# A two-layer graph network: row sums on quarters of TensorE's array, edge products on halves of it

## The chip, the core and the metric

One Trainium2 chip, one of its cores. A core has five engines that run side by side: TensorE (PE, matrix products into PSUM; its weight loads are PEld), VectorE (DVE), ScalarE (ACT), GpSimd (POOL, which here issues the indirect DMAs, that is gathers and scatters by an index list) and SyncE (SP, which issues the plain DMAs). The metric is the time of one execution in microseconds (us).

## What is computed

A graph of 1250 nodes with 512 features and 40000 edges, sorted by target node. First layer: graph attention with 8 heads of 64 features, then a dense block. Second layer: edge features are mixed into the messages, which are summed, then two dense layers with a normalisation over the nodes. Cut to what matters:

```python
# first layer
h  = layer_norm(x) * ln1_g + ln1_b
xl, xr = (h @ Wl).reshape(-1, 8, 64), (h @ Wr).reshape(-1, 8, 64)
e  = einsum('ehc,hc->eh', leaky_relu(xl[src] + xr[dst], 0.2), att)
ex = exp(e - segment_max(e, dst)[dst])
alpha = ex / (segment_sum(ex, dst)[dst] + 1e-16)
x1 = x + segment_sum(alpha[..., None] * xl[src], dst).reshape(-1, 512) + gat_bias
x1 = x1 + gelu((layer_norm(x1) * ln2_g + ln2_b) @ W1 + b1) @ W2 + b2
x  = layernorm(x + x1)
# second layer
msg = relu(x[src] + edge_attr @ W_e + b_e)
h   = (1 + eps) * x + segment_sum(msg, dst)
h   = silu(batch_norm(h @ W1 + b1)) @ W2 + b2
out = layernorm(x + silu(batch_norm(h)))
```

All of it is in float32.

## The kernel before

**Blocks and rows.** The nodes are ranked by degree and put in ten blocks of 128, one node per SBUF partition. Block b has `KB[b]` slots (44 in block 0 down to 25 in block 9, 333 in all). One slot of a block is one gathered "row": a POOL instruction (`get`, `gather`) that fetches, for each of the 128 nodes, the 512 features of its neighbour in that slot. Each layer gathers 333 such rows.

**Recorded order.** In the first layer and the preparation all engines are called through `inorder`, which makes the instructions of an engine run in the order of the program. All those instructions carry one line, L783, so they are told apart by their tiles. The second layer's edge part calls the engines directly and has lines of its own.

**Preparation** (to about 85 us): weights are turned and permuted, the left features `xl` are written to a table in HBM, ranks and index lists are made. Its last steps turn the permutation that is to be undone later (`pu_` into `undo`), permute the bias (`pg`), form the last block's product (`product(9)`, `taken(9)`, `lin(8, 9)`), and form the negated right features of block 9 (`xn` to `xT` to `nxr9`).

**First layer, attention** (about 100 to 905 us). A block's rows come in groups of at most 20 (`GN`), 21 groups, and a group in chunks of at most 5 rows (`CN`), 75 chunks. A chunk has one buffer `xg`; there are seven (`GB`). For each chunk, in the loop over groups and chunks:

- `scores`: POOL gathers the chunk's rows into `xg`; DVE takes maximum and minimum with `nxr` into `z`, multiplies by a sign and reduces to the scores `S`. After a group's last chunk `softmax` forms the weights `w`.
- `weigh`, for one chunk of the group before: ACT multiplies about half of the rows by the weights, head by head, DVE the other rows in one product (`xg<-xg,w`); `add_up` then sums the rows, one PE matmul per row with the identity as weights, into the PSUM tile `pacc` (two buffers). Between the rows' sums `part` puts a step of another block's dense layer (`body_of`).
- `merge`, one group later still, adds the group's sum to the block's accumulator `acc` with the softmax correction.
- At a block's first group `normed_of` gathers the next block's node rows into `xn` (one buffer) at the end of the first chunk, and `xr_of`, from the third chunk on, makes the next `nxr` (two buffers) of it. `slots_of` gathers the next block's index list `s_n`.

A chunk's `xg` buffer is free for new gathers when the sums of its rows are done.

**Dense block of the first layer.** `head_of` normalises and turns a finished block, `body_of` does 16 pairs of products: `pu` (four 128x128 matmuls, then GELU on ACT into `uT`) and `py` (one 128x512 matmul, accumulated in PSUM; two buffers), with `end_of` to add, normalise and scatter the result. Their steps are dealt out by `part`, `step_others` and `step_lates`; what remains is done behind the attention (the tail, about 905 to 985 us).

**Second layer, edge part** (about 985 to 1460 us). The features of a block's edges come in one or two gathers `ea` of at most 28 slots (`spans`, `features_of`). `turn` transposes eight slots at a time, two per 128 partitions. `edges` handles rows in pairs: POOL gathers two rows `xs`; PE forms both edge products `pe`, each from all 128 partitions with a weight tile `we` whose other half is zero; DVE adds `pe` to `xs` (L1747) and, in a second instruction, takes the maximum with 0 and adds to the sum `pd` in PSUM (L1748). Between pairs `first_dense` does the next dense layer for finished blocks (`pz`, L1704). `pe` has two buffers, `xs` nine.

**End** (to 1578 us): normalisations over nodes, second dense layer, scatter of the output.

A second function, `general_path`, is compiled beside it for inputs that this plan does not cover. It doesn't run here.

Of the kernel before, what the change touches and what calls it, by code (L numbers as in the profile page):

```python
# [725 lines left out]
def gnn_kernel(ctx, tc, x, src, dst, edge_attr, ln1_g, ln1_b, Wl, Wr, att, gat_bias,  # L726
# [44 lines left out]
    def inverse_std(rs, var):  # L771

        nc.scalar.activation(rs, var, AF.Sqrt, bias=ln_eps[:rs.shape[0]])
        nc.vector.reciprocal(rs, rs)
# [40 lines left out]
    with ExitStack() as s0:  # L815
# [121 lines left out]
        orders = [order, *(kl.tile([P, KD, P], F32, name=f"order{i}") for i in range(2))]  # L937
# [251 lines left out]
        pu_ = lq.tile([P, KD, P], F32, name="pt1")  # L1189
        for k in range(KD):  # L1190
            T.transpose(pu_[:, k, :], orders[2][:, k, :], ident)
        A.copy(sgn, q_b.rearrange("p (h c) -> p h c", c=CH)[:, :, LEFT:RIGHT])
        A.copy(undo, pu_)
        pg = kq.tile([P, KD], F32, name="pg", tag="s")
        for k in range(KD):
            T.matmul(pg[:, k:k + 1], order[:, k, :], cols[:, 68 + k:69 + k], start=True, stop=True)
        A.copy(gcols, pg)
        A.mul(ncols, cols[:, 52:60], -1.0)
# [3 lines left out]

        pt = lq.tile([P, KD, P], F32, name="pt1")
        for k in range(KD):
            T.transpose(pt[:, k, :], xn[:, k * P:(k + 1) * P], ident)
        for k in range(KD):
            A.activation(xT[:, k, :], pt[:, k, :], AF.Identity,
                         scale=ncols[:, k:k + 1], bias=ncols[:, KD + k:KD + k + 1])
# [9 lines left out]
        A.copy(nxr9[:, :, 1:], pm.rearrange("p k n -> p (k n)").rearrange("p (h c) -> p h c", c=CH))  # L1218

    def short_path():  # L1220
        with ExitStack() as sa:
            fast = sa.enter_context(tc.tile_pool(name="fast", bufs=1))
            fdram = sa.enter_context(tc.tile_pool(name="fdram", bufs=1, space=DRAM))
            xb_t = fdram.tile([N + 1, D], F32, name="xb_t")
            xo_t = fdram.tile([NP, D], F32, name="xo_t")
            eps1 = row(eps, 1, "eps1", fast)
            nc.vector.tensor_scalar(eps1, eps1, 1.0, None, op0=OP.add)
            back = fast.tile([P, P], F32, name="back")
            nc.vector.tensor_scalar(back, jp, float(-V0), None, op0=OP.is_equal)
            lone = fast.tile([P, 1], F32, name="lone")  # L1230
            nc.vector.tensor_scalar(lone, jp[:, 0:1], float(-VN), -0.1 * BIG, op0=OP.is_le, op1=OP.mult)
            s2 = sa.enter_context(ExitStack())
            early = {}
            with ExitStack() as s1:
                V, A, T = attention(s1, xb_t, xo_t, back, lone, lambda: begin(s2, early))
            second(s2, early, xb_t, xo_t, eps1, back, V, A, T)

    def attention(s1, xb_t, xo_t, back, lone, follow):
# [26 lines left out]
        V.memset(one, 1.0)  # L1265
        w1 = ap.tile([P, KD, FF], F32, name="w1")
# [35 lines left out]
        def xr_of(blk):  # L1302

            yield from place()
            pt = aq.tile([P, KD, P], F32, name="pt1", tag="pu", bufs=4)
            for k in range(KD):
                T.transpose(pt[:, k, :], blk["xn"][:, k * P:(k + 1) * P], ident)
            yield
            xT = bp.tile([P, KD, P], F32, name="xT", tag="t")
            for k in range(KD):  # L1310
                A.activation(xT[:, k, :], pt[:, k, :], AF.Identity,
                             scale=ncols[:, k:k + 1], bias=ncols[:, KD + k:KD + k + 1])
            held["ps"] -= 1
            yield from place()
            pm = aq.tile([P, D], F32, name="pm", tag="pu", bufs=4)
            for k in range(KD):
                T.matmul(pm, xT[:, k, :], wr[:, k, :], start=(k == 0), stop=(k == KD - 1))
            yield
            blk["nxr"] = nxr = bp.tile([P, HEADS, CX], F32, name="nxr", bufs=2)
            A.copy(nxr[:, :, 1:], heads(pm))  # L1320
            held["ps"] -= 1
            V.memset(nxr[:, :, 0:1], -NEG)
# [24 lines left out]
        held = dict(acc=0, hT=0, head=0, h=0, ps=0)  # L1347
# [62 lines left out]
        def body_of(b, y, hT):  # L1410

            py = aq.tile([P, D], F32, name="py", bufs=2)
# [20 lines left out]
        def end_of(b, y, py):  # L1433

            yield
            V.tensor_add(y, y, py)
            xo = bp.tile([P, D], F32, name="xo")
# [35 lines left out]
        def part():  # L1473

            if not going and ready:
                going.append(body_of(*ready.pop(0)))
            if going and next(going[0], 0) == 0:
                going.pop()
# [44 lines left out]
        def add_up(g, j):  # L1523
            T.matmul(heads(g["pacc"]), ident, row_of(g, j), start=(j == 0), stop=(j == g["n"] - 1))

        def weigh(g):
# [4 lines left out]
            g["pacc"] = aq.tile([P, D], F32, name="pacc", bufs=2)  # L1531
            for c, (c0, cn) in enumerate(g["cuts"]):
# [3 lines left out]
                for j in range(c0, c0 + cn):  # L1536
                    if j < c0 + na:
                        xv = row_of(g, j)
                        for h in range(HEADS):
                            A.activation(xv[:, h, :], xv[:, h, :], AF.Copy, scale=w[:, j, h:h + 1])  # L1540
                    if g["quota"] > 0:
                        g["quota"] -= 1
                        part()
                    add_up(g, j)
                yield

# [56 lines left out]
        for i, g in enumerate(groups):  # L1603
# [9 lines left out]
            g["S"] = sp.tile([P, GN + 1, HEADS], F32, name="S")  # L1613
            nc_ = len(g["cuts"])
            for c in range(nc_):
# [3 lines left out]
                if c == 0:  # L1619
                    if not i:  # L1620
                        others.append(wr_order())
                    if g["first"] and g["b"] != ORDER[-1]:
                        others.append(slots_of(g["b"] - 1))
                        ahead = normed_of(g["b"] - 1)
# [3 lines left out]
                if c == min(1, nc_ - 1) and merging:  # L1628
                    merge(merging)
                if c == 2 and g["first"] and ahead:  # L1630
                    others.append(xr_of(ahead))
                step_others()
                todo = 0
# [3 lines left out]
                for _ in range(todo):  # L1637
                    before["quota"] = quota
                    next(weighing, 0)
                    quota = before["quota"]  # L1640
                for _ in range(quota):
                    part()
                step_lates()
            merging, before = before, g
        merge(merging)
# [4 lines left out]
        follow()  # L1650
        merge(before)
# [6 lines left out]
    def begin(s2, early):  # L1658
# [3 lines left out]
        early["we"] = we = er.tile([P, 2, D], F32, name="we")  # L1662
        nc.gpsimd.memset(we, 0.0)
        nc.sync.dma_start(we[0:ED, 0, :], W_e)
        nc.sync.dma_start(we[ED:P, 1, :], W_e)
        early["features"] = [features_of(ep, *u) for u in spans[:2]]
# [5 lines left out]
    spans = [(b, e0, en) for b in (NB - 1, *range(NB - 1)) for e0, en in parts(KB[b], 28)]  # L1672

    def features_of(ep, b, e0, en):

        wx = w_i[:, b:b + 1]
        if e0:
            wx = ep.tile([P, 1], I32, name="wx")
            nc.vector.tensor_scalar(wx, w_i[:, b:b + 1], float(e0), None, op0=OP.add)
        ea = ep.tile([P, 28 * ED], F32, name="ea", bufs=3)  # L1680
        gather(ea[:, :en * ED], edge_attr, wx)
        return ea

    def second(s2, early, xb_t, xo_t, eps1, back, V, A, T):
# [25 lines left out]
        with ExitStack() as s3:  # L1710
# [3 lines left out]
            pend = {u: ea for u, ea in zip(spans, early["features"])}  # L1714

            def turn(b, e0, en, c0, cn, act=nc.scalar):

                at = spans.index((b, e0, en))
                if c0 == 0:
                    for u in spans[at:at + 2]:  # L1720
                        if u not in pend:
                            pend[u] = features_of(ep, *u)
                ea = pend[b, e0, en]
# [12 lines left out]
            def edges(b, at0, cn, eaT, pd):  # L1736
                for j in range(0, cn, 2):
# [4 lines left out]
                    pe = eq.tile([P, 2, D], F32, name="pe")  # L1742
                    for i in range(m):
                        kk = P if m == 2 else ED
                        nc.tensor.matmul(pe[:, i, :], eaT[:kk, j // 2, :], we[:kk, i, :], start=True, stop=True)  # L1745
                    xv = xs[:, :m, :]
                    add = nc.vector.tensor_add(xv, xv, pe[:, :m, :])  # L1747
                    nc.vector.scalar_tensor_tensor(pd[:, :m, :], xv, 0.0, pd[:, :m, :], op0=OP.max, op1=OP.add)  # L1748
                    if at0 == KO[NB - 1] and j == 2:
                        for k in (NB - 1, *range(NB - 1)):  # L1750
# [15 lines left out]
            units = [(b, e0, en, c0, min(8, en - c0)) for b, e0, en in spans for c0 in range(0, en, 8)]  # L1766
            todo, work = [], None
            eaT = turn(*units[0], A)
            for n, (b, e0, en, c0, cn) in enumerate(units):
                if e0 == 0 and c0 == 0:  # L1770
# [4 lines left out]
                    else:  # L1775
                        (nc.vector if n else V).memset(pd, 0.0)
                ahead = turn(*units[n + 1], nc.scalar if n else A) if n + 1 < len(units) else None
                for _ in edges(b, KO[b] + e0 + c0, cn, eaT, pd):
# [5 lines left out]
                if e0 + c0 + cn == KB[b]:  # L1784
# [131 lines left out]
```

## Time and profile before

| | |
|---|---|
| median of 17 runs | 1579.13 us (1571.07 to 1583.69) |
| profiled execution | 1580.21 us |
| its span, first to last instruction | 1578.4 us |
| mean granted TensorE clock | 0.911 |
| busy: PE, PEld, DVE, ACT, POOL | 1291.4, 673.5, 1177.4, 655.7, 817.5 us |
| row sums `pacc<-xg,ident` | 666 passes, 373.8 us busy, 136.9 us idle before them |
| row gathers `xg`, then `xs` | 333 each, 408.8 and 314.9 us busy on POOL |
| edge products `pe<-we,eaT` | 666 passes, 329.1 us busy |

How to read it: a group is one kind of instruction, `out<-in`, with its count and busy time; "idle before, releaser" is time in which the engine stood, and what ended it. A float32 matmul appears as two passes, each with its weight load. Matmuls overlap their neighbours' ends, so the mean of one is longer than the distance between starts. A wait for several things is put down to the one that came last by the profile, which can be wrong where that engine had long been done. The chain of waits is followed back from the last instruction.

### The profile page before, as it was taken

Reading aid. Unit: us, or ns where it says so; the run is one execution under the profiler, and the core shown is the slowest. Engines: PE = TensorE matmul, PEld = TensorE weight load, DVE = VectorE, ACT = ScalarE, POOL = GpSimd, SP = SyncE. Lnnn points to the kernel's source line nnn. Section 1 sums busy time; section 2 is a strip of 40 time slices with the busy share of each in tenths; the row PEclk is TensorE's granted clock in tenths of the full one; section 3 lists DMA queues with packets and bytes.
Section 4 is the critical chain, followed back from the end, with each engine's and each line's share of the span. In section 5 each row is a group of like instructions: output and inputs, shape, how many; then the busy total and the mean of one; then the engine's idle time right before and its main releaser. Section 6 shows DMA issues by size and latency. Waiting matters only on the chain.

```text
span 1578.4 us, 14337 instructions
## 1 busy us (share of the span) xinstructions
PE 1291.4 (82%) x4290; PEld 673.5 (43%) x4290; DVE 1177.4 (75%) x1494; ACT 655.7 (42%) x1980; POOL 817.5 (52%) x762
## 2 busy tenths in 40 slices
PE   7836668979889798887969898888878999898893
PEld 4422224545545354443525465333323354344552
DVE  7768798687787778789796511899999789969133
ACT  5425365557756556666657542000000111011433
POOL 2368565544464646474664101777777767743002
PEclk9968678989999899897989999899999999999897
DMA  6257754323443534454443131877777767743001
GB/s 234 70 158 249 258 149 112 106 82 108 120 124 112 146 99 139 115 149 116 120 138 108 57 128 51 279 236 212 225 224 224 217 182 212 225 136 108 0 0 67
DMA packets 74597, 228.66 MB, mean 145 GB/s; under 512 B 14750, under 2 KB 15236, under 8 KB 73999
## 3 DMA queue, kind: packets, MB, share of 16 engines
q0 software_dynamic: 60000, 199.10, 42.9%
q1 hardware_dynamic: 14511, 28.56, 5.0%
q8 instruction: 36, 0.59, 0.1%
q14 instruction: 50, 0.41, 0.1%
HBM read 214.68 MB, written 13.05 MB: 144 GB/s over the span
## 4 chain that ended last, share of the span: by engine, by line
PE 41%; DVE 20%; issue 13%; DMA 11%; ACT 10%; POOL 4%; POOLq 0%; DVEq 0%; SPq 0%; ACTq 0%
PE pacc L783 14%; PE pu L783 6%; DVE pd L1748 5%; ACT xg L783 5%; PE pz L783 5%; PE py L783 5%; DMA xs<-xb_t,src_i 5%; DVE z L783 4%; PE pe L1745 4%; DMA xg<-xl_t,src_i 3%; DVE xs L1747 3%; DVE S L783 3%; PE pm L783 3%; PE pz L1704 3%; POOL xs L749 2%
## 5 line engine op out<-in xcount | busy, mean ns | idle before, releaser
L783 POOL DMA_INDIRECT xg<-xl_t,src_i x333 | 408.8, 1228 | 340.5 <-issue 190.1
L783 PE MATMUL pacc<-xg,ident 128*128 128x512 f32 x666 | 373.8, 685 | 136.9 <-ACT xg L783 126.7
L749 POOL DMA_INDIRECT xs<-xb_t,src_i x333 | 314.9, 946 | 126.7 <-issue 65.8
L1745 PE MATMUL pe<-we,eaT 128*128 128x512 f32 x666 | 329.1, 626 | 36.5 <-DVE xs L1747 35.6
L783 ACT ACTIVATE xg<-xg,w 128x64 f32<-128x64 f32 x1328 | 329.0, 341 | 0.0
L783 DVE TENSOR_TENSOR z<-xg,nxr 128x1440 f32<-128x1440 f32 (+4 forms) x150 | 197.1, 1355 | 110.5 <-DMA xg<-xl_t,src_i 110.4
L783 PEld LDWEIGHTS pacc<-xg,ident 128*128 128x128 f32 x666 | 134.2, 215 | 327.9 <-ACT xg L783 202.8
L1747 DVE TENSOR_TENSOR xs<-xs,pe 128x1024 f32<-128x1024 f32 (+1 forms) x170 | 202.1, 1191 | 33.0 <-DMA xs<-xb_t,src_i 19.5
L1745 PEld LDWEIGHTS pe<-we,eaT 128*128 128x128 f32 x666 | 120.4, 197 | 203.6 <-issue 108.3
L783 PEld LDWEIGHTS pu<-hT,w 128*128 128x128 f32 x1280 | 173.3, 200 | 74.7 <-issue 65.7
L1748 DVE SCALAR_TENSOR_TENSOR pd<-xs,pd 128x1024 f32<-128x1024 f32 (+1 forms) x170 | 203.9, 1199 | 1.3
L783 DVE TENSOR_REDUCE S<-z 128x40 f32<-128x2600 f32 (+2 forms) x75 | 191.8, 2558 | 2.6
L783 PE MATMUL pu<-hT,w 128*128 128x128 f32 x1280 | 176.8, 284 | 0.2 <-DVE oacc L783 0.2
L783 PE MATMUL py<-w,uT 128*128 128x512 f32 x320 | 163.7, 596 | 0.0
L783 ACT ACT_TABLE_LOAD x71 | 91.1, 1283 | 30.7 <-DVE S L783 24.3
L783 DVE TENSOR_TENSOR xg<-xg,w 128x1024 f32<-128x1024 f32 (+2 forms) x75 | 99.9, 1335 | 0.0
L783 ACT ACTIVATE uT<-pu,cols 128x128 f32<-128x128 f32 x160 | 56.3, 363 | 96.9 <-PE pu L783 96.0
L1731 ACT COPY eaT<-pt 128x512 f32<-128x512 f32 (+3 forms) x44 | 23.5, 534 | 173.0 <-PE pe L1745 145.6
L783 DVE TENSOR_TENSOR z<-z,sgn 128x960 f32<-128x960 f32 (+2 forms) x75 | 77.8, 1038 | 0.0
L783 PE MATMUL pz<-z,v 128*128 128x512 f32 (+1 forms) x192 | 71.1, 530 | 6.0 <-ACT z L783 6.0
L741 POOL DMA_INDIRECT out_dram<-z,v_i x10 | 10.0, 1002 | 123.0 <-ACT z L783 120.5
L1704 PE MATMUL pz<-hT,v 128*128 128x512 f32 (+3 forms) x256 | 70.6, 418 | 0.4 <-ACT z L1706 0.4
(268 smaller groups left out, 1002.5 us busy)
## 6 DMA issues: line engine op xcount, KB each, us to landing
w<-in_L_gnn_W_dram SPq DMA_DIRECT2D x8, 1024.0 KB
xg<-xl_t,src_i POOLq DMA_INDIRECT x333, 3.7
xs<-xb_t,src_i POOLq DMA_INDIRECT x333, 3.7
v<-in_L_gnn_W_dram SPq DMA_DIRECT2D x2, 2048.0 KB
xo_t<-xo SPq DMA_DIRECT2D x10, 256.0 KB
x_out<-xo_t SPq DMA_DIRECT2D x10, 256.0 KB
xl_t<-xo SPq DMA_DIRECT2D x9, 260.0 KB
hn_t<-hn SPq DMA_DIRECT2D x9, 256.0 KB
```

Of the source, the lines that this page charges most:

```text
L741: s = nc.gpsimd.indirect_dma_start(out=table, out_offset=bass.IndirectOffsetOnAxis(ap=idx, axis=0), in_=rows, in_offset=None, bounds_check ...
L749: return nc.gpsimd.indirect_dma_start(out=rows, out_offset=None, in_=table, in_offset=bass.IndirectOffsetOnAxis(ap=idx, axis=0))
L783: ins = getattr(engine, name)(*args, **kw)
L1704: T.matmul(pz[:, :nn], v1[:, k, f * P:(f + 1) * P], hT[:, k, n0:n0 + nn], start=(k == 0), stop=(k == KD - 1))
L1731: act.copy(eaT[:, :full, :], pt[:, :full, :])
L1745: nc.tensor.matmul(pe[:, i, :], eaT[:kk, j // 2, :], we[:kk, i, :], start=True, stop=True)
L1747: add = nc.vector.tensor_add(xv, xv, pe[:, :m, :])
L1748: nc.vector.scalar_tensor_tensor(pd[:, :m, :], xv, 0.0, pd[:, :m, :], op0=OP.max, op1=OP.add)
```

## The change

- **Row sums.** Each row is summed by two 64x64 matmuls instead of one 128x128: its upper 64 partitions into one PSUM bank of the tile `sums`, its lower 64 into the other. Rows alternate between the lower and the upper half of the output partitions, so that four positions of the array are in use. The order alternates rows from the chunk's end (DVE's) and from its start (ACT's). All parts of a chunk now come before its sums.
- **Folding.** A group's sums stand in four places. ACT copies both banks to SBUF (`taken`: `ab0`, which takes `xn`'s buffer, and `ab1`), and two matmuls with a stacked identity `fold` add the halves into `pacc` (`folded`).
- **Room.** `sums` has one buffer of two banks, `pacc` and `py` one each; `part` starts a body only when `py` is free. `S` has two buffers. Odd blocks keep their right features in `nxr9`, even ones in one `nxr`. The gather of `xn` moves behind the second chunk's gathers.
- **Edge products.** The weights stand once in each half of the partitions; the two products of a pair use one half each. For every third full pair PE also adds the gathered rows (two matmuls with the identity), ACT takes the maximum with 0, and DVE only adds to `pd`. Edge features come in one gather per block.
- **Preparation.** `xn` is turned ahead of `product(9)`; the undoing order and the bias come last. Two tables move to another pool. `inverse_std` of this function, which nothing on the path calls, is written differently.

```diff
@@ preparation
+        pt = lq.tile([P, KD, P], F32, name="pt1")
+        for k in range(KD):
+            T.transpose(pt[:, k, :], xn[:, k * P:(k + 1) * P], ident)
+        A.mul(ncols, cols[:, 52:60], -1.0)
+        for k in range(KD):
+            A.activation(xT[:, k, :], pt[:, k, :], AF.Identity,
+                         scale=ncols[:, k:k + 1], bias=ncols[:, KD + k:KD + k + 1])
         product(9)
         taken(9)
         lin(8, 9)
...
@@ attention
+    H2 = P // 2
...
+        fold = ap.tile([P, H2], F32, name="fold")
+        V.tensor_add(fold, ident[:, 0:H2], ident[:, H2:P])
...
-            blk["nxr"] = nxr = bp.tile([P, HEADS, CX], F32, name="nxr", bufs=2)
+            blk["nxr"] = nxr = bp.tile([P, HEADS, CX], F32, name="nxr") if blk["b"] % 2 == 0 else nxr9
...
-            py = aq.tile([P, D], F32, name="py", bufs=2)
+            py = aq.tile([P, D], F32, name="py")
+            held["py"] = 1
...
-            if not going and ready:
+            if not going and ready and not held["py"]:
...
-        def add_up(g, j):
-            T.matmul(heads(g["pacc"]), ident, row_of(g, j), start=(j == 0), stop=(j == g["n"] - 1))
+        def add_up(g, j, i):
+
+            row = row_of(g, j)
+            for k in range(2):
+                r = slice(k * H2, k * H2 + H2)
+                T.matmul(heads(g["sums"][i * H2:i * H2 + H2, k, :]), ident[r, r], row[r], start=not g["at"][i],
+                         stop=g["at"][i] == g["rows"][i] - 1)
+            g["at"][i] += 1
...
-            g["pacc"] = aq.tile([P, D], F32, name="pacc", bufs=2)
+            g["sums"] = aq.tile([P, 2, D], F32, name="sums")
...
                     if g["quota"] > 0:
                         g["quota"] -= 1
                         part()
-                    add_up(g, j)
+                while g["quota"] > 0:
+                    g["quota"] -= 1
+                    part()
+                for j in range(cn):
+                    add_up(g, c0 + j // 2 if j % 2 else c0 + cn - 1 - j // 2, j % 2)
                 yield
 
+        def taken(g):
+
+            g["ab"] = [bp.tile([P, D], F32, name="ab0", tag="xn"), bp.tile([P, D], F32, name="ab1")]
+            for k in range(2):
+                A.copy(g["ab"][k], g["sums"][:, k, :])
+
+        def folded(g):
+            g["pacc"] = pacc = aq.tile([P, D], F32, name="pacc")
+            for k in range(2):
+                T.matmul(pacc[k * H2:k * H2 + H2, :], fold, g["ab"][k], start=True, stop=True)
...
-                        ahead = normed_of(g["b"] - 1)
...
+                if c == 1 and g["first"] and g["b"] != ORDER[-1]:
+                    ahead = normed_of(g["b"] - 1)
                 if c == 2 and g["first"] and ahead:
                     others.append(xr_of(ahead))
                 step_others()
+                if c == 0 and merging:
+                    taken(merging)
                 todo = 0
...
+                if c == 0 and merging:
+                    folded(merging)
                 for _ in range(quota):
                     part()
...
@@ second layer
-        early["we"] = we = er.tile([P, 2, D], F32, name="we")
-        nc.gpsimd.memset(we, 0.0)
-        nc.sync.dma_start(we[0:ED, 0, :], W_e)
-        nc.sync.dma_start(we[ED:P, 1, :], W_e)
-        early["features"] = [features_of(ep, *u) for u in spans[:2]]
+        early["we"] = we = er.tile([P, D], F32, name="we")
+        nc.sync.dma_start(we[0:ED, :], W_e)
+        nc.sync.dma_start(we[ED:P, :], W_e)
+        early["features"] = [features_of(ep, b) for b in BLOCKS[:2]]
...
                     pe = eq.tile([P, 2, D], F32, name="pe")
+                    pairs[0] += 1
+                    by_pe = pairs[0] % 3 == 0 and m == 2
                     for i in range(m):
-                        kk = P if m == 2 else ED
-                        nc.tensor.matmul(pe[:, i, :], eaT[:kk, j // 2, :], we[:kk, i, :], start=True, stop=True)
+                        r = slice(i * ED, i * ED + ED)
+                        nc.tensor.matmul(pe[:, i, :], eaT[r, j // 2, :], we[r, :], start=True, stop=not by_pe)
                     xv = xs[:, :m, :]
-                    add = nc.vector.tensor_add(xv, xv, pe[:, :m, :])
-                    nc.vector.scalar_tensor_tensor(pd[:, :m, :], xv, 0.0, pd[:, :m, :], op0=OP.max, op1=OP.add)
+                    if by_pe:
+                        for i in range(m):
+                            nc.tensor.matmul(pe[:, i, :], ident, xs[:, i, :], start=False, stop=True)
+                        nc.scalar.activation(xv, pe, AF.Relu)
+                        nc.vector.tensor_add(pd, xv, pd)
+                    else:
+                        add = nc.vector.tensor_add(xv, xv, pe[:, :m, :])
+                        nc.vector.scalar_tensor_tensor(pd[:, :m, :], xv, 0.0, pd[:, :m, :], op0=OP.max, op1=OP.add)
```

## The prediction

> **What bounds the kernel now.** I read the page first (shares, slices, chain), then the groups and waits of the attention stage alone, then engine by engine the order of time in one block, and last POOL's own order of time in the second layer.
>
> ```profile
> PE 1291.4 (82%) x4290; PEld 673.5 (43%) x4290; DVE 1177.4 (75%) x1494; ACT 655.7 (42%) x1980; POOL 817.5 (52%) x762
> ...
> PE 41%; DVE 20%; issue 13%; DMA 11%; ACT 10%; POOL 4%; POOLq 0%; DVEq 0%; SPq 0%; ACTq 0%
> PE pacc L783 14%; PE pu L783 6%; DVE pd L1748 5%; ACT xg L783 5%; PE pz L783 5%; PE py L783 5%; DMA xs<-xb_t,src_i 5%; DVE z L783 4%; PE pe L1745 4%; DMA xg<-xl_t,src_i 3%; DVE xs L1747 3%; DVE S L783 3%; PE pm L783 3%; PE pz L1704 3%; POOL xs L749 2%
> ```
>
> No engine fills the span, and the row sums (`pacc`) head the chain with 14%, some 226 us. That share is an average of two stages. The attention stage (about 100 to 905 us) has these waits, first and third the ones to see:
>
> ```profile
> POOL xg L783 <- ACT xg L783: 88.8, 24, 11.4
> PE pacc L783 <- ACT xg L783: 126.7, 44, 12.1
> DVE z L783 <- DMA xg<-xl_t,src_i: 105.1, 28, 9.4
> ```
>
> POOL has no free `xg` buffer, so DVE waits for rows. In order of time, POOL, then DVE, then PE around one such place:
>
> ```profile
> 517.74 1.85 POOL L783 DMA_INDIRECT xg<-xl_t,src_i  x1 [3.51 <-ACT xg L783]
> ...
> 527.93 2.39 DVE L783 TENSOR_TENSOR z<-xg,nxr 128x1440 f32<-128x1440 f32 x2 [4.07 <-DMA xg<-xl_t,src_i]
> ...
> 522.08 1.02 PE L783 MATMUL pacc<-xg,ident 128*128 128x512 f32 x2
> ...
> 524.69 1.88 PE L783 MATMUL pacc<-xg,ident 128*128 128x512 f32 x4
> ```
>
> I tabulated the stage's 75 chunks. From the 26th to the 71st, each chunk's gathers start 0.9 us (median) after the row sums of the chunk seven places earlier end: the seven buffers are a ring. Its means: last sum to gather 0.9, gather to `z` 10.7, `z` to the scores' end 6.2, from there to the weighing product of the chunk four places earlier 1.4, and from that product to the end of its row sums 13.5. Together 32.7 us for 7-4=3 chunks, 10.9 a chunk; measured 10.7. So this ring sets the pace, with DVE (about 80% busy) not far behind, and a microsecond off a chunk's row sums is worth a third of one.
>
> In the second layer POOL stands like this, row after row:
>
> ```profile
> 1116.51 0.95 POOL L749 DMA_INDIRECT xs<-xb_t,src_i  x1 [0.30 <-issue]
> 1117.76 0.95 POOL L749 DMA_INDIRECT xs<-xb_t,src_i  x1 [0.30 <-issue]
> 1119.01 0.94 POOL L749 DMA_INDIRECT xs<-xb_t,src_i  x1 [0.30 <-issue]
> ```
>
> One gather every 1.25 us, without a gap from 980 to 1264 us. DVE needs 2.26 us for the pair of rows that takes POOL 2.5. The bound here is the issue of gathers. Only where the dense layer's `pz` falls between (around 1251 to 1290 and 1370 to 1413) is PE the bound: 8 passes of `pe` and 8 of `pz` in 6.87 us.
>
> **The change, part by part.** The profiled execution took 1580.21 us (span 1578.4), 1.1 above the median of 1579.13.
>
> *Row sums on quarters.* A row's sum now takes two passes of 0.43 us (back-to-back starts), 0.86. After, it is two 64x64 matmuls, four passes. No row of the trace shows two matmuls on separate parts of the array. The nearest:
>
> ```profile
> L1745 PE MATMUL pe<-we,eaT 128*128 128x512 f32 x634 | 313.6, 626 | 35.2 <-DVE xs L1747 34.3 <-ACT eaT L1731 0.6
> L1745 PE MATMUL pe<-we,eaT 64*128 64x512 f32 x12 | 6.7, 641 | 1.0 <-DVE xs L1747 1.0
> ```
>
> Half the height saves nothing by itself, so a row costs 1.72 us if quarters take turns and 0.43 if four run at once; two at once is 0.86 again. I take 0.43: the matmuls carry four disjoint positions, their outputs lie in separate banks and partition halves, and the rows are dealt so that neighbours alternate. This is the weakest step, and both ends stay in the range. A change of shape costs 0.19: `py<-b,one` (1 row high) to the next `pu` is 1.05 us where full-height passes take 0.86. With 333/75=4.44 rows a chunk: 4.44x0.43-0.19=1.7 us sooner, a third of it times 75 is 43 us. In each block's first group PE runs chunk after chunk without a gap (16 to 20 us from product to last sum), where the gains add up over chunks, up to 75 us in all. I take -58.
>
> The Trainium skill, "TensorE: Matmul & The Clock Gate", Part 3, lets matmuls on different tiles start about 4 ns apart, but also says that matmuls start strictly in program order. The trace shows two passes per fp32 matmul, one behind the other on the same weights; by that rule the second pass would hold the next quarter back, two would run at a time, and the sum would be the second rival's 1645 instead of the forecast. No run here shows which holds.
>
> *Folds and copies.* 21 groups each add two folding matmuls (0.86 with both column halves at once, plus 0.19; 1.48 with the passes two at a time) and two PSUM copies on ACT (0.58 each, row of `acc<-pacc`). ACT reaches the copies before the next group's scaling, so both lie on the ring at a group's first chunk: 21x1.05/3=+7 and 21x1.16/3=+8.
>
> *The queue on POOL.* `ab0` takes the buffer of `xn`. So the gather of the next block's `xn`, moved behind the second chunk's gathers, waits for the fold, and on POOL the third chunk's row gathers stand behind it. It happens in 8 blocks. In the block shown, those gathers start at 517.74; the sums that stand before the fold end at 526.4, then come fold and `xn` (1.05+1.25): 11 us later, and DVE is already waiting there (4.07). Sooner sums shorten it to some 7, and the next two chunks, whose buffers are free by then, give part back. I take 3 a block, +24; bounds 0 and 88.
>
> *Other moves in this stage.* `py` has one buffer: the next body waits for DVE's addition, and by the order of the code six `py` and three `pu` steps more remain for the tail (6x0.86+3x0.89=8 us of PE; there 4.6 us were idle): +4, bounds 0 and 8. Parts now precede a chunk's sums instead of alternating; the last sum came after the last part before too: nothing. `S` with two buffers, `nxr9` in turn with one `nxr`, and one DVE addition for `fold` cost nothing while a group's scores are read before the group after next, which the order of the code gives; if not, a DVE wait of microseconds. The new `inverse_std` isn't called on this path.
>
> *Preparation.* `xn`'s transposes come before `product(9)`, which waited 4.54 us behind `pg`: it can start 2 us sooner, but the first `xg` now waits for the transposes of the undoing order, last on PE. -0.7, bounds -2 and +2.
>
> *Second layer.* 18 feature gathers become 10, with more bytes each: 8x1.25=-10 on POOL, the bound. 163 pairs run on halves; 54 of them add rows on PE (1.72), with a ReLU on ACT (about 1.0, from 0.58 for half the size; ACT is 10% busy) in place of a DVE instruction of 1.21: 65 us less on DVE, which didn't bind. Average PE per pair: 0.86+0.19+0.57=1.62 at two halves at once, 1.72 before: so the dense stretches stay. DVE catches up sooner after them: the last gather to the last addition was 17.8 us, I take 10 (-8), and -2 for POOL's stalls. Sum -20. Best: 980.1 plus 340 issues of 1.252 plus 10 is 1416 against 1459, -43. Worst, halves in turn, +50. On the third pairs PE waits for the gathered rows, and the next pair's products and `pz` stand behind it; the nine `xs` buffers cover that while POOL is ahead.
>
> Sum: -58+7+8+24+4-0.7-20=-36 from 1580.2, **1544 us**.
>
> **The rivals.**
>
> 1. The POOL queue decides (slower). Place: the `xn` gather behind the fold; price: the full 11 us in 8 blocks, 88 instead of 24: 1608. Above 7.5 us a block it outweighs the rest. For it: DVE waits for exactly these gathers today. Against: DVE then runs at its own 8.6 us a chunk with buffers in hand, and wins some back.
> 2. Two at a time (slower). Sums cost PE what they did, plus one pass (0.43) and the switch per chunk: 0.62/3x75=+15; folds 21x1.48/3=+10; copies +8; queue +24; tail +6; second layer 1.29+0.19+0.57=2.05 a pair, +0.33 over some 60 pairs in dense stretches, less 18: +2. 1645. For it: the passes of one matmul follow each other in the trace without overlap.
> 3. No overlap: the part isn't what its name says. 333x0.86=286 us more PE in a stage where its starts fill some 615 of 805 (666+256+72 passes of 0.43, 1024 of 0.139, some 45 for the rest): about +170, and +50 in the second layer, about 1800. Against: the disjoint positions.
>
> **How the numbers follow.** Forecast 0.47 (its own range 1500 to 1573), rival 1 0.15, rival 2 0.25, rival 3 0.13. Leaving out rival 3 and the very best end gives 1490 to 1660. A difference under 0.2% can't be told from none here. Faster takes the forecast's case less 0.03 near zero: 0.44; same 0.05 (with 0.02 of rival 1); slower 0.51, the rest of the rivals. The likeliest single case is still a gain.
>
> **What would show it.** Starts of `sums` passes: quarters 0.1 us apart or less and ten in about 2.6 us (forecast), 0.43 apart (rival 2 shows 0.43 for each two), 0.43 for each (rival 3). POOL waiting before `xn<-hn_t,v_c` with the fold as releaser, 8 times, and DVE's `z` waiting behind it: 7 or more net is rival 1. In the second layer gathers still 1.25 us apart, the last addition near 1440. I'm wrong beyond all of this if PE's clock, 0.91 granted, falls because PE idles more, or if a mode change costs far more than 0.19 us.

## The result, and the profile after

The changed kernel takes 1607.46 us (median of 8 runs, 1605.55 to 1613.38), the kernel before 1579.06 (46 runs): ratio 1.0191, 95% interval 1.0172 to 1.0210. It is 1.9% slower, where the forecast was 1544 us. The first rival, POOL's queue, had given 1608.

The profiled execution of the changed kernel took 1607.39 us, its span is 1605.6, its granted TensorE clock 0.881. From its page: busy times, the chain that ended last, and the groups of the two changed products (busy us, mean ns, then idle before them):

```profile
PE 1228.0 (76%) x5256; PEld 583.0 (36%) x5256; DVE 1123.9 (70%) x1433; ACT 737.6 (46%) x2082; POOL 804.8 (50%) x753
...
POOL 0%; issue 0%; POOLq 0%
POOL out_dram L741 0%; POOLq L1952 0%; POOLq L1923 0%
...
L782 PE MATMUL sums<-xg,ident 64*64 64x512 f32 x1332 | 239.5, 743 | 114.8 <-DVE xg L782 75.5
...
L1775 PE MATMUL pe<-we,eaT 64*128 64x512 f32 x666 | 205.0, 665 | 48.5 <-DVE xs L1783 47.1
```

PE is busy for 63 us less, and the row sums went from 373.8 us to 239.5 although their passes doubled. The chain tells nothing this time: it breaks off after the last scatter, for a reason that comes at the end of the experiments. So the stages have to be compared instead, from the first and last starts of their instructions in both traces (us):

| stage | before | after | difference | predicted |
|---|---|---|---|---|
| start to first `xg` gather | 83.9 | 83.0 | -0.9 | -0.7 |
| first `xg` gather to first row sum | 36.0 | 36.5 | +0.5 | 0 |
| first row sum to end of the last | 780.4 | 805.9 | +25.5 | -19 |
| to first `xs` gather (tail) | 79.9 | 87.2 | +7.3 | +4 |
| first to last `xs` gather | 461.0 | 443.9 | -17.1 | -12 |
| to end of last addition to `pd` | 17.8 | 23.2 | +5.4 | -8 |
| to end of span | 119.5 | 125.9 | +6.4 | 0 |

The loss lies in the stage of the row sums, and there not in the sums. Waits of this stage in the changed kernel (100 to 905 us; us in total, times, longest):

```profile
DVE z L782 <- DMA xg<-xl_t,src_i: 125.3, 23, 16.6
...
PE sums L782 <- DVE xg L782: 75.5, 18, 21.9
POOL xn L782 <- issue: 74.9, 4, 26.7
...
POOL xn L782 <- ACT acc L782: 54.4, 4, 19.2
...
POOL xg L782 <- ACT xg L782: 32.3, 8, 6.7
...
PE sums L782 <- ACT xg L782: 19.3, 25, 3.1
```

The two waits that headed the list before are small now: POOL waiting for a free `xg` buffer fell from 88.8 to 32.3, PE waiting for ACT's scaled rows from 126.7 to 19.3. In their place POOL stands 129.3 us before eight `xn` gathers, DVE's wait for gathered rows grew from 105.1 to 125.3, in fewer and longer pieces, and PE stands 75.5 us for DVE's weighed rows. One of the eight in order of time, on PE, ACT, POOL and DVE (start, duration, then idle before it and releaser):

```profile
634.15 1.95 PE L782 MATMUL sums<-xg,ident 64*64 64x512 f32 x16
636.03 1.08 PE L782 MATMUL pacc<-ab,fold 128*64 128x512 f32 x4
```

```profile
637.18 0.59 ACT L782 COPY acc<-pacc 128x512 f32<-128x512 f32 x1 [3.58 <-PE pacc L782]
```

```profile
624.91 1.40 POOL L782 DMA_INDIRECT xg<-xl_t,src_i  x1 [0.30 <-issue]
637.85 0.94 POOL L782 DMA_INDIRECT xn<-hn_t,v_c  x1 [11.53 <-ACT acc L782]
639.09 0.95 POOL L782 DMA_INDIRECT xg<-xl_t,src_i  x1 [0.30 <-issue]
...
642.84 0.95 POOL L782 DMA_INDIRECT xg<-xl_t,src_i  x1 [0.30 <-issue]
```

```profile
635.96 1.21 DVE L782 TENSOR_TENSOR xg<-xg,w 128x1024 f32<-128x1024 f32 x1
646.57 2.45 DVE L782 TENSOR_TENSOR z<-xg,nxr 128x1440 f32<-128x1440 f32 x2 [9.40 <-DMA xg<-xl_t,src_i]
```

The fold ends at 637.1, ACT's copy of `pacc` into `acc` behind it at 637.8, and with this copy's signal `xn` goes out at 637.85 (so the releaser is named as ACT's `acc`; the buffer was written by ACT and read by the fold). The third chunk's four rows are issued from 639.09 to 642.84. DVE has finished everything else at 637.2 and stands 9.40 us until they have landed. The same wait follows each of the eight `xn` gathers, 8.6 to 16.6 us long, 95.9 us in all. In the kernel before, DVE's waits for the rows of the same eight chunks sum to 16.1 us.

The 16 passes of the first PE line show how quarters run. Their starts in the trace are 634.149, .156, .162, .169, then four from 634.629 on, four from 635.058, four from 635.487: four passes at a time, 6 to 7 ns apart, and the next four 0.43 us later (the first step 0.48). A row costs 0.43, the forecast's value. The two products of a pair in the second layer start 7 ns apart too.

The granted clock was full in these 2 us. In this trace it is either full or half, and where it was half (0.50 in the 3.7 us of the next line) a step of four passes takes 0.85 to 0.91 us:

```profile
401.52 3.69 PE L782 MATMUL sums<-xg,ident 64*64 64x512 f32 x16
```

In the whole stage 140 steps take under 0.5 us at full clock and 70 take 0.83 to 0.93 at half. So the forecast's 0.43 holds for most rows, not for all.

### The profile page after: what moved, and what is told of

Its sections match the earlier page's. It is cut to its first block, busy times and chain, and to the rows that moved or that the text cites. A ratio compares the mean times of both kernels' runs of the same rounds, so it can differ in the third digit from the quotient of the medians.

```text
span 1605.6 us, 16369 instructions
## 1 busy us (share of the span) xinstructions
PE 1228.0 (76%) x5256; PEld 583.0 (36%) x5256; DVE 1123.9 (70%) x1433; ACT 737.6 (46%) x2082; POOL 804.8 (50%) x753
## 5 line engine op out<-in xcount | busy, mean ns | idle before, releaser
L782 PE MATMUL sums<-xg,ident 64*64 64x512 f32 x1332 | 239.5, 743 | 114.8 <-DVE xg L782 75.5
L1775 PE MATMUL pe<-we,eaT 64*128 64x512 f32 x666 | 205.0, 665 | 48.5 <-DVE xs L1783 47.1
L782 PE MATMUL py<-w,uT 128*128 128x512 f32 x320 | 174.9, 638 | 43.7 <-ACT uT L782 41.2
L1780 ACT ACTIVATE xs<-pe 128x1024 f32<-128x1024 f32 x54 | 55.2, 1023 | 261.8 <-PE pe L1779 239.4
L782 PEld LDWEIGHTS sums<-xg,ident 64*64 64x64 f32 x1332 | 62.4, 158 | 278.9 <-issue 85.2
L1783 DVE TENSOR_TENSOR xs<-xs,pe 128x1024 f32<-128x1024 f32 (+1 forms) x116 | 135.8, 1181 | 21.7 <-DMA xs<-xb_t,src_i 19.0
L1784 DVE SCALAR_TENSOR_TENSOR pd<-xs,pd 128x1024 f32<-128x1024 f32 (+1 forms) x116 | 138.4, 1193 | 2.6
L1779 PE MATMUL pe<-xs,ident 128*128 128x512 f32 x216 | 115.8, 659 | 10.1 <-DMA xs<-xb_t,src_i 9.7
L1775 PEld LDWEIGHTS pe<-we,eaT 64*128 64x128 f32 x666 | 56.9, 191 | 146.6 <-DVE xs L1783 77.8
L1781 DVE TENSOR_TENSOR pd<-xs,pd 128x1024 f32<-128x1024 f32 x54 | 66.3, 1229 | 54.0 <-ACT xs L1780 50.1
L782 DVE TENSOR_TENSOR z<-z,sgn 128x960 f32<-128x960 f32 (+2 forms) x75 | 77.9, 1038 | 0.0
```

Source lines behind the costliest of these rows:

```text
L782: ins = getattr(engine, name)(*args, **kw)
L1775: nc.tensor.matmul(pe[:, i, :], eaT[r, j // 2, :], we[r, :], start=True, stop=not by_pe)
L1779: nc.tensor.matmul(pe[:, i, :], ident, xs[:, i, :], start=False, stop=True)
L1780: nc.scalar.activation(xv, pe, AF.Relu)
L1781: nc.vector.tensor_add(pd, xv, pd)
```

## The experiments

In the twelve later runs (the last four on another chip than the eight before) the kernel before takes 1666 to 1671 us instead of 1579, since gathered rows land later. In the second layer, where DVE had waited over 1 us for a pair of rows, the pair's last gather had been issued 5.5 us earlier in the first measurement (median of 8 cases) and 16.9 us earlier in the run f1_first_own (30 cases), whose second layer is that of before. In each of the nine longest of these 30 waits the edge product had ended 3.3 us or more before DVE went on, so the rows came last. PE's clock is lower in this stretch too (0.96 before, 0.88 in f1_first_own): PE was busy at half clock for 32 and 86 us of it, which can have cost some 27 us of the 85 that the stretch grew by (an estimate: half of the difference). Whether the late rows lie in the chips or in something else about these runs they don't tell. DVE's waits in the second layer, first in the kernel before, then in f1_first_own; "remote" is a signal whose sender the profile can't name:

```profile
DVE xs L1747 <- DMA xs<-xb_t,src_i: 19.5, 13, 7.7
```

```profile
DVE xs L1782 <- remote: 66.0, 13, 9.1
```

So each ratio is against the kernel before on the same chip in the same round, and gains and losses in us are that ratio on its median. The stages of one profiled execution each (us); the first two lines are the first measurement:

| kernel | row sums | tail | `xs` gathers | to last addition | to end | ratio (95%) |
|---|---|---|---|---|---|---|
| before | 780.4 | 79.9 | 461.0 | 17.8 | 119.5 | 1 |
| after | 805.9 | 87.2 | 443.9 | 23.2 | 125.9 | 1.0191 |
| g0_after_here | 806.8 | 88.7 | 543.4 | 23.8 | 126.0 | 1.0304 (1.0249 to 1.0358) |
| e3_first_only | 806.8 | 89.9 | 541.4 | 21.5 | 119.3 | 1.0227 (1.0193 to 1.0260) |
| e2_second_only | 778.7 | 78.0 | 554.8 | 27.7 | 126.6 | 1.0101 (1.0057 to 1.0144) |
| f3_queue_only | 851.8 | 79.4 | 542.9 | 20.5 | 119.5 | 1.0408 (1.0376 to 1.0441) |
| e1_own_buffer | 728.1 | 85.6 | 535.5 | 23.9 | 126.1 | 0.9826 (0.9777 to 0.9875) |
| e1b_xn_early | 728.0 | 87.1 | 545.4 | 23.9 | 126.0 | 0.9824 (0.9773 to 0.9874) |
| f2_both_memset | 724.5 | 85.6 | 548.8 | 28.9 | 125.5 | 0.9852 (0.9805 to 0.9900) |
| f1_first_own | 723.1 | 90.4 | 545.6 | 20.3 | 119.6 | 0.9697 (0.9666 to 0.9728) |
| f1_again | 728.6 | 90.0 | 538.4 | 20.6 | 119.4 | 0.9740 (0.9686 to 0.9793) |
| f4_halves_only | 779.7 | 77.9 | 539.8 | 21.8 | 126.8 | 0.9981 (0.9951 to 1.0011) |
| g4_own_halves | 727.5 | 87.2 | 543.6 | 21.9 | 126.3 | 0.9760 (0.9709 to 0.9811) |
| g1_eight_gathers_back | 727.4 | 87.2 | 533.5 | 22.1 | 119.4 | 0.9665 (0.9614 to 0.9717) |

The stage of the row sums is the same in both (805.9 and 806.8 for the changed kernel; 780.4, and 778.7 and 779.7 where the first layer is that of before), so it can be compared across them.

**The shared buffer taken away.** The theory: what costs is the gather of `xn` behind the fold on POOL. The rival: copies, folds, the new order of parts or a lower clock.

```diff
-            g["ab"] = [bp.tile([P, D], F32, name="ab0", tag="xn"), bp.tile([P, D], F32, name="ab1")]
+            g["ab"] = [bp.tile([P, D], F32, name="ab0", tag="t"), bp.tile([P, D], F32, name="ab1")]
...
-            xT = bp.tile([P, KD, P], F32, name="xT", tag="t")
+            xT = bp.tile([P, KD, P], F32, name="xT", tag="xn")
```

> The changed kernel, but the copy `ab0` no longer shares a buffer with the gathered node rows `xn` (it takes that of `t`, and `xT` moves to that of `xn`), so that the gather of `xn` doesn't wait for the fold. Nothing else differs. Theory (POOL's queue): the 127 us that POOL stands before eight `xn` gathers go, the third chunk's row gathers come with their buffers, and the stage of the row sums falls from 806 to some 730-750 us; in all about 1540 (1525-1560). Rival (copies, folds, the new order of parts, or PE's lower clock hold the stage): the POOL stall turns into another wait, 1595-1610.

1636.14 us against 1665.65, 29 us faster than before, and the stage of the sums is 728.1 us, 78 less than in the changed kernel. Its waits in that stage (100 to 860 us):

```profile
DVE z L782 <- DMA xg<-xl_t,src_i: 55.0, 25, 4.4
...
POOL xg L782 <- ACT xg L782: 46.2, 11, 8.4
...
POOL xn L782 <- issue: 2.1, 7, 0.3
```

POOL no longer stands before `xn`, and DVE's waits for rows fall from 125.3 to 55.0 us, none above 4.4. The rival is out for copies, folds and order of parts: they are all still there. The clock did rise with the wait gone: in the stage of the sums it is 0.90 in the kernel before, 0.84 in the changed one and 0.88 here, and PE was busy at half clock for 121.3, 174.8 and 146.5 us of it. If half of such time is lost, the lower clock cost PE some 14 us more with the wait than without (an estimate). Of the 78 us it can explain no more than that.

With the `xn` gather back behind the first chunk:

```diff
                     if g["first"] and g["b"] != ORDER[-1]:
                         others.append(slots_of(g["b"] - 1))
+                        ahead = normed_of(g["b"] - 1)
...
-                if c == 1 and g["first"] and g["b"] != ORDER[-1]:
-                    ahead = normed_of(g["b"] - 1)
```

> As the run before, and the gather of `xn` back behind the first chunk's gathers, where the kernel before has it. Theory: the place of the gather costs nothing once it waits for nothing, so the same as that run within 5 us. Rival (the later `xn` makes the next block's right features late): 5 to 15 us faster than that run.

1639.18 us, the same. The later place costs nothing; the wait does.

**The wait alone, in the kernel before.**

```diff
             get(blk["xn"], hn_t, v_c[:, b:b + 1])
+            if summed[0] is not None:
+                after(ins, [summed[0]], "behind the row sums")
...
+                if c == 1 and g["first"] and g["b"] != ORDER[-1]:
+                    ahead = normed_of(g["b"] - 1)
```

(`ins` is this gather, `summed[0]` the last `add_up` so far; the call of `normed_of` at the first chunk is gone.)

> The kernel before with one thing of the change alone: the gather of `xn` stands behind the second chunk's gathers and waits for the row sums that precede the fold in the changed kernel. No quarters, no fold, no copies. Theory: POOL stands 10 to 26 us before eight of these gathers, the third chunk's rows come late: +60 to +100 us. Rival (the wait costs only because all parts now come before a chunk's sums): under +20.

1739.81 us, 68 us slower; the stage of the sums is 71 to 73 longer (851.8 against 778.7 to 780.4). POOL's waits in it:

```profile
POOL xn L783 <- PE pacc L783: 61.0, 5, 12.7
...
POOL xn L783 <- PE px L783: 49.0, 2, 29.7
...
POOL xn L783 <- PE pu L783: 25.9, 1, 25.9
```

Eight waits, 135.9 us, with no quarter, fold or copy in the kernel. DVE's waits behind the eight gathers are 8.5 to 18.2 us, 101.3 in all. So the wait costs nearly as much beside the old sums (71 to 73 us of the stage) as beside the quarters (78).

**Each part alone, and both here.** The kernel of before with the functions from `begin` on taken from the changed one, and the other way round.

```diff
+        early["we"] = we = er.tile([P, D], F32, name="we")
+        nc.sync.dma_start(we[0:ED, :], W_e)
+        nc.sync.dma_start(we[ED:P, :], W_e)
+        early["features"] = [features_of(ep, b) for b in BLOCKS[:2]]
...
```

> The kernel before with the second layer's part alone (halves, every third pair by PE, one feature gather per block). Theory: the stretch of `xs` gathers falls by 17 us as in the changed kernel, its end gives 5 back and the end of the program 6: about 1574 (-5), 1568 to 1578. Rival (the second layer's loss at its ends comes from the first layer's tail, not from this part): -15 to -20, about 1562.

1686.62 us: 17 us slower, which neither side expected. The two losses at the ends, some 7 us each, remain. The stretch of gathers itself takes 554.8 us, no less than with the old second layer (538 to 546): where DVE waits for landing rows the saved issues are worth nothing that shows. That this is the reason is argued from the stretch alone.

> The kernel before with the first layer's part and the new order of the preparation alone. Theory: stage of the sums +25, tail +7, preparation -1: 1579+31=1610 (1604-1615). If the two parts work on each other, the two single runs' differences don't add up to the +28 of both.

1704.59 us, 38 slower where 31 was expected; the stage is 806.8.

> The changed kernel as it is, on the chip of these runs, for the sum of the parts. If the two parts' differences add up (first layer +39 us, second layer +17 where the gathers of the second layer land late): about 1.033 on that chip; on a chip like that of the first measurement 1.019. If the parts work on each other: off the sum by 10 us or more.

1722.49 us, 51 slower; 17 and 38, from the other chip, make 55, inside the interval (42 to 60). The two parts don't work on each other by an amount that these runs can tell.

**The first layer's part without the wait**, second layer as before:

> The kernel before with the first layer's part and the new preparation, where `ab0` doesn't share `xn`'s buffer; the second layer as before. Theory: the two runs before this give the first layer's part +39 us with the shared buffer; the wait of `xn` is worth some 78 of it (the stage of the sums was 807 with it, 728 without), so about -40 us, ratio 0.975 (0.970 to 0.981). Rival (the two parts gain only together): -10 or less.

1620.92 us, ratio 0.9697, and in another round:

> The first layer's part with `ab0` apart from `xn`, second layer as before, again as the yardstick of the next two: 0.970 on the same chip; on a chip where gathers land sooner also about 0.97 (-50 us), since the gain lies in the first layer.

1628.43 us, 0.9740. The quarters are worth some 43 to 51 us of the whole, and the stage is 723.1 and 728.6 us against 780.4: -52 to -57 for sums, folds and copies, where -43 was predicted.

**The end of the program.** In every kernel with the second layer's part, but for the last one tried here, the time after the last `pd` addition is 6 to 7 us longer, although PE, ACT and DVE do the same work there. What differs is POOL's closing drain, a sequencer instruction that isn't counted as busy. Its row on the line of the launch (durations min/median/max in ns) in before and after:

```profile
L1912 POOLq DRAIN  x3: 40/113/3628, 1573.7 to 1578.1; - x3
```

```profile
L1952 POOLq DRAIN  x3: 44/113/12622, 1592.1 to 1605.3; - x3
```

3.6 us against 12.6; from the end of the last scatter's issue to the end of the span it is 3.3 against 10.0. Two things differ on POOL: a memset of `we` is gone, and there are 746 indirect DMAs instead of 754. First the memset, put back on an unused tile in the kernel of e1:

```diff
+        zero = er.tile([P, 2 * D], F32, name="zero")
+        nc.gpsimd.memset(zero, 0.0)
```

> The changed kernel with `ab0` in a buffer of its own kind, and a POOL memset of one tile (nothing reads it) where the kernel before clears the upper halves of `we`. It tests why POOL's closing drain took 12.6 us in every kernel with the second layer's part and 3.7 in the others. If the memset is what shortens it: drain back to 3.7, the last scatter to the end 3.4 us, 6.5 us less than the run without it, ratio about 0.979. If it depends on the count of gathers, which is 8 fewer: drain still 12.6, ratio as in that run, 0.983.

The drain stays at 12.5 us; 1641.95 us, ratio 0.9852, not different from e1_own_buffer. It isn't the memset. Then the gathers:

```diff
+        junk = er.tile([P, 8, 8], F32, name="junk")
+        for k in range(8):
+            gather(junk[:, k, :], edge_attr, w_i[:, k:k + 1])
```

> The run above plus eight small gathers that nothing reads, issued in the first layer's tail where POOL stands idle some 70 us. If the closing drain depends on the number of gathers: drain 3.7 instead of 12.6, last scatter to end 3.4, so 6.5 us less than the run above. If it depends on something else of the second layer's part: 12.6 as there, and the same time within 3 us.

```profile
L1955 POOLq DRAIN  x3: 44/113/3605, 1611.2 to 1615.5; - x3
```

Back at 3.6 us, 3.2 from the last scatter's issue to the end. The yardstick without the eight gathers:

> The run above plus halves and one feature gather per block, no pair added by PE. Theory: where the second layer is held by landing gathers its stretch stays, and the longer closing drain takes 6.6 us: 0.970 to 0.973; where it is held by POOL's issues, 10 to 17 us off the stretch less 6.6: 0.963 to 0.968.

There it is 12.6 and 9.9, and 1634.48 us against 1617.96 with them. (Its ratio of 0.9760 lies above both expectations; against f1_again it is 6 us, the drain's size, though the intervals overlap.) 6.7 of the 16.5 us are the end of the program; 10.1 lie in the stretch of `xs` gathers of the two profiled executions (543.6 and 533.5), which varies by 7 between kernels with the old second layer (538.4 to 545.6) and by 19 between those with the whole new one (535.5 to 554.8), so this part is open. What about the count decides, its size or its remainder by something, these two values can't tell.

**Every third pair.** The halves and the single feature gathers without the pairs that PE and ACT add:

```diff
-                    by_pe = pairs[0] % 3 == 0 and m == 2
+                    by_pe = False
```

> The kernel before with the second layer's halves and one feature gather per block, but no pair added up by PE and ACT, and the POOL memset kept. Theory (the every third pair's longer chain, products, rows added by PE, ReLU, addition, makes the end late): last gather to last addition back to 17.8 us from 23-28, gathers' stretch as before or shorter, ratio 0.995 to 1.000. Rival (the end is late because gathers no longer pause for features): 23 us or more here too, 1.003 to 1.008.

The ratio is 0.9981: the same as before, 20 us less than e2_second_only. Last gather to last addition is 21.8 us, close to the later runs with the old second layer (20.3 to 21.5), and 27.7 with the third pairs. Over all later runs it is 20.3 to 22.1 without them and 23.8 to 28.9 with them. The end is late because of them, not because gathers pause less. DVE's lines near the end, in the changed kernel as first measured, show how:

```profile
1460.00 1.23 DVE L1781 TENSOR_TENSOR pd<-xs,pd 128x1024 f32<-128x1024 f32 x1 [3.33 <-DMA xs<-xb_t,src_i]
...
1468.37 1.23 DVE L1781 TENSOR_TENSOR pd<-xs,pd 128x1024 f32<-128x1024 f32 x1 [2.04 <-ACT xs L1780]
...
1474.92 1.23 DVE L1781 TENSOR_TENSOR pd<-xs,pd 128x1024 f32<-128x1024 f32 x1 [0.66 <-ACT xs L1780]
```

A third pair goes through PE, ACT and DVE one after the other, and DVE takes pairs in order: 6.0 us of waits in the last 20. (For the first of them the profile names the DMA, but ACT's maximum for that pair ended at 1459.96, just before.) Over the whole stage DVE stands 54.0 us before these additions, against 5.4 us that the end grew: most of it seems to be hidden while POOL issues. With the first layer's part beside it the cost of the third pairs can't be told from none (e1_own_buffer 0.9826, g4_own_halves 0.9760, the intervals overlap).

**The best version** here is g1_eight_gathers_back: 1617.96 us, 0.9665 of before, 6% less than the changed kernel beside it. The highest of its four runs (1619.4) is under the lowest of f1_again (1625.2). How it stands where gathers land as in the first measurement wasn't tried; by the stages, the changed kernel without the wait would be some 1607-79=1528 there, an estimate.

## Why the prediction was wrong

**The step that failed is the term of POOL's queue: +24 taken, 79 to 81 measured** (the stage of the sums 806.8 against 728.1 for both parts; 806.8 against 725.9, the mean of two, for the first layer's alone). The mechanism was named, its place and releaser too, and the upper bound of 88 held. Wrong were two sizes: the delay, which sooner sums were to shorten to some 7 us, and what "the next two chunks" give back of it, from which the 3 us a block came. DVE's waits behind the eight gathers average 12.0 us, and the loss is 10, above the 7.5 from which the rival was to decide.

Where the waits come from can be read from the lines above. The fold stands behind the sums of a chunk that DVE has to weigh first, and when it ends DVE has just finished the scores of the group's second chunk and has no third one in SBUF. Then come ACT's copy (0.6 us), `xn` (1.25), four or five gathers (1.25 each) and the landing, 8.6 us or more with DVE idle, in every block. POOL's lead over DVE, which seven buffers are there to give, is used up once per block. How far POOL had run ahead only shows in how long POOL stands (9.8 to 26.7 us).

What is given back differs between the first half and the second. From the first sum to those of the 26th chunk the kernel before takes 277.6 us, the changed one 305.5, e1_own_buffer 251.0; from there to the last 502.6, 500.3 and 476.9. So the wait cost 54.5 us in the first stretch, with four of the `xn` gathers and 55.7 us of DVE's waits behind them: all of it. In the second it cost 23.4 of 40.1, some 6 a block. The prediction's example lay in the second stretch, and its 3 was half of what that stretch showed; the first was not looked at. There DVE has no slack to win anything back with: without the wait it is busy for 212.6 of the 230 us from 100 to 330, against 221.5 of the 270 after them. That this is why is argued, not shown. In f3_queue_only the two stretches lose about alike, 40.0 of 56.4 us of DVE's waits and 31.4 of 44.9. And the clock is a second candidate: in the first stretch PE was busy at half clock for 82.2 us with the wait and 54.3 without (some 14 us lost, estimated as above), in the second for 92.6 and 92.2.

In the ring of the 26th to 71st chunk the same is seen from outside: the part from weighing product to last sum fell from 13.5 to 9.5 us, the step from the last sum to the next gather grew from 1.0 to 3.9, the one from gather to `z` from 10.7 to 11.6, and the period stayed 10.73. Without the wait it is 10.26.

The other terms:

- Row sums, folds and copies, -58+7+8=-43: measured -52 to -57 without the wait. Right in size, and four at a time. The Trainium skill, "TensorE: Matmul & The Clock Gate", Part 3, has two statements here. That tiles start about 4 ns apart is near the trace, which has 6 to 7 ns; the trace decides. That matmuls start strictly in program order would have given two at a time if the second pass of a product stood directly behind the first; four start together, so either the passes stand in another order or they don't start in program order. The records name neither the pass nor its weights, and no run here tells which.
- Tail +4: +7.3. In the tail PE runs 80 passes of `py` instead of 68 and 280 of `pu` instead of 256, the six and three steps predicted; their 8 us weren't absorbed by PE's idle time. The upper bound was right.
- Preparation -0.7: -0.9.
- Second layer -20: -5.3 in the first measurement. The stretch of gathers fell as predicted and by more (-17.1 against -12): 8 feature gathers stand in it instead of 15, and POOL's idle time over the 0.3 us ahead of every issue fell from 27.1 to 19.1 us. "DVE catches up sooner" (-8) was wrong by sign: +5.4, since the third pairs put PE and ACT before DVE in series. The closing drain (+6.4) wasn't seen at all; its 3.6 us in the kernel before gave no sign that it would grow.
- Rival 2 (two at a time) and rival 3 (no overlap) are refuted by the starts of the passes. Rival 1's 1608 is met, and for its reason: 80 where it had 88. That the number fits to a microsecond is partly luck, since the sums gave 9 to 14 us more than it held and the second layer 15 less.
- The lower clock, named as a danger, came (0.911 to 0.881), most of it in the stage of the sums (0.90 to 0.84). It isn't free: at half clock a step of the sums takes 0.85 us instead of 0.43. It doesn't decide either: e1_own_buffer has 0.88 in this stage, under the 0.90 of before, and is 52 us faster in it.

## What to carry to other kernels

A wait added to one instruction of an in-order queue is charged to everything behind it, and buffers further on pay little of it back while that queue is the one that fills them (here nothing in one stretch, 16.7 of 40.1 us in the other): price it as the delay at the first consumer, in every stretch of the program by that stretch's own slack. Sharing a buffer between a gather and a late product is such a wait, though the code shows none; two tags exchanged turned 3% slower into 2% faster (on two chips, each against the kernel before on its own). And a saving in issues counts only where issues are the bound; in the later runs DVE waited for the landing of gathers, and eight issues fewer brought nothing that shows.

## What the runs showed that was not expected

POOL's closing drain took 12.5 to 12.6 us in the eight profiled executions with 746 indirect DMAs and 3.6 to 3.7 in the six with 754; eight tiny gathers in idle time took 6.7 us off the end. And the kernel before differed by 5.7% between the first measurement and the later runs (1579.06 and 1669.38 us), nearly all of it in the second layer: the stage of the row sums agrees to 2 us, the stretch of `xs` gathers is 461 us in the one and 538 to 546 in the others with the same second layer.
